# Splitting the 3x3 matmuls of convolutions 1 and 3 by row blocks, unshifted blocks first

## The chip, the cores and the metric

The kernel runs on one core of a Trainium2 chip. The metric is the time of one execution on the device, in microseconds, and the median of several runs is quoted. Besides the times there is one profiled execution, with a record of every instruction, DMA packet and semaphore update. All the readings below come from it.

A core has a matrix engine (TensorE, "PE" in the profile, with its weight loads under "PEld"), a vector engine (VectorE, "DVE"), an activation engine (ScalarE, "ACT"), a general engine (GpSimd, "POOL") and SyncE ("SP"), which here issues DMAs. Matmul results go to PSUM. Everything else lives in SBUF, which has 128 partitions.

## The reference

The input `x` has shape (8, 32, 128, 128). Two layers add to it. The first is a denoiser:

```
xb   = patch_match_stack(groupnorm(x))                   # 8 best shifted copies: 256 channels
dct  = conv(xb, dct_w, groups=32)
h    = relu(conv3x3_dw(conv1x1(xb, w1), w2))             # convolution 1
h    = relu(conv3x3_dw(conv1x1(h,  w3), w4))             # convolution 2
wien = sigmoid(conv3x3_dw(conv1x1(h, w5), w6))           # convolution 3
x    = x + conv1x1(conv(wien * dct, inv_dct_w, groups=32), agg_w)
```

`conv3x3_dw` is a 3x3 convolution that treats each of the 256 channels by itself, with a border of zeros. The second layer normalises again and adds a 5x5 convolution. The change concerns `conv3x3_dw` of convolutions 1 and 3.

## The kernel before, in words

**Tiles and steps.** An image is worked in 16 tiles of 8 rows (`R`), and a 17th short tile for the last rows, because each 3x3 convolution works one row behind its input. There are 8 x 17 = 136 steps (`steps`). In step `s` the kernel runs convolution 1 for tile `s`, convolution 2 for tile `s - 1`, convolution 3 for tile `s - 2` and the final stage for tile `s - 2`. Inside a step the loop goes `for i in (3, 2, 1, 0)`; 0 is the final stage. The same step also gathers pixels for later tiles and prepares the next image, whose VectorE tasks are dealt out by `tick`.

**Two halves of the channels.** Channels 128 to 255 take their 3x3 convolution on VectorE (`depthwise_v`, L695, nine taps). Channels 0 to 127 take it on TensorE (`depthwise_t`, L718), and that is the part that changes. Its 1x1 convolution (`pointwise_t`, L665) writes, through a ScalarE copy (L672), into the buffer `t`, one for each convolution, of 128 partitions x 4 channel groups x 4 slots x 128 columns. A partition stands for one of 4 rows and one of 32 channels. The ScalarE copy fills slots 2 and 3. A 3x3 convolution needs neighbouring rows on the partitions that one matmul contracts over, so slots 0 and 1 hold the same rows moved by half the partitions. DMAs on SyncE's queue fill them:

- L677, `t[64:P, :, 0:2] <- t[0:64, :, 2:4]`, of this tile;
- L679, `t[0:64, :, 1] <- t[64:P, :, 2]`, of this tile;
- L620 (`rows_before_t`), `t[0:64, :, 0] <- t[64:P, :, 3]`, issued after the convolution for the next tile.

**The matmuls.** `depthwise_t` reads `t` as two row blocks: block 0 is slots 0 and 1 (the shifted ones), block 1 is slots 2 and 3 (the unshifted ones). For each of two output offsets `u` (0 contracts over 96 partitions, 1 over 128), three column taps `dx` and four channel groups `j`, one matmul takes both blocks together, 2 x 2 x 128 = 512 columns (508 for the side taps). That makes 24 matmuls in the code; the trace shows each as two, 48 for one call. `pt[0]` and `pt[1]` are two PSUM buffers (`ps_dw`, one of each), read by two ScalarE activations (L731).

**Where a call stands.** `depthwise_t` is a generator. Its matmuls run at the first `next(dt)` of the iteration after its own, so that other work stands between the DMAs and their readers. On TensorE a full step goes: `pv3, p3, pg, | pv2, p2, pg, [3x3 of conv 3] | pv1, p1, pg, [3x3 of conv 2] | pc, pg, [3x3 of conv 1]`, where `pv` and `p` are the 1x1 convolutions (L641, L665), `pg` the gathered pixels (L603), `pc` the DCT (L777), and small pieces (`pd`, `pa`, `px`, `pt`) are put between. TensorE, VectorE and ScalarE run in exactly the order in which the code issues (`manual_schedule`). GpSimd's and SyncE's queues are ordered by the framework's scheduler.

Of the kernel before, what the change touches and what calls it, by code (L numbers as in the profile page):

```python
# [15 lines left out]
P = 128  # L16
C, K, H, W = 32, 8, 128, 128
# [3 lines left out]
NS = H // R  # L21
# [21 lines left out]
def bm3d_conv_preact(  # L43
# [16 lines left out]
    nc = tc.nc  # L60
# [49 lines left out]
    dwd = const.tile([P, 3, 2, 4, 3, C], F32, name="dwd")  # L110
# [36 lines left out]
    with tc.tile_pool(name="setup", bufs=1) as sp, tc.tile_pool(  # L147
# [23 lines left out]
        for name, w in (("w1", w1), ("w3", w3), ("w5", w5)):  # L171
            t = sp.tile([P, 2, CK], F32, name=f"nat_{name}", tag=f"nat_{name}")
            nc.sync.dma_start(t, w.rearrange("(m p) i a b -> p m (i a b)", p=P))
            if name == "w1":

                nat, t = t, sp.tile([P, 2, CK], F32, name="w1_kc")
# [439 lines left out]
    def rows_before_t(i, b, n):  # L616

        t = tb[i - 1]
        if n < NS:
            nc.sync.dma_start(t[0:64, :, 0], t[64:P, :, 3])  # L620
        else:
            nc.gpsimd.memset(t[0:64, :, 0], 0.0)
# [80 lines left out]
    def depthwise_t(i, b, n):  # L703
        t = tb[i - 1].rearrange("p q (h k) w -> p q h k w", k=2)
        nb = 2 if n < NS else 1

        pt = [
            ps_dw.tile([P, 2, 2, W], F32, name=f"pw{i}_{b}_{n}_{u}", tag=f"dw{u}")
            for u in range(2)
        ]  # L710

        nh = [2 if n < NS else (i + 1 - u) // 2 for u in range(2)]
        for u in range(2):
            hi = 96 if u == 0 else P
            for dx in (0, -1, 1):
                xa, xz = max(0, -dx), min(W, W - dx)
                for j in range(4 if nh[u] else 0):
                    nc.tensor.matmul(  # L718
                        pt[u][C * j : C * (j + 1), : nh[u], :nb, xa:xz],
                        dwd[0:hi, i - 1, u, j, dx + 1],  # L720
                        t[0:hi, j, : nh[u], :nb, xa + dx : xz + dx],
                        start=dx == 0,
                        stop=True,
                        skip_group_check=True,
                    )
        yield 1
        acc = accp.tile([P, R, W], F32, name=f"acc{i}_{b}_{n}_0", tag=f"acc{i}0")
        rows = acc.rearrange("p (k e) w -> p e k w", e=4)
        for u in range(2):
            if nh[u]:  # L730
                nc.scalar.activation(  # L731
                    rows[:, u : u + 2 * nh[u] - 1 : 2, :nb], pt[u][:, : nh[u], :nb], funcs[i - 1]
                )
        rows_before_t(i, b, n)
        accs[i, b, n][0] = acc
# [263 lines left out]
    with tc.manual_schedule(engines=ORDERED):  # L999
# [9 lines left out]
        u = 4  # L1009
# [5 lines left out]
        for s in range(len(steps) + 2):  # L1015
            if s < len(steps):
                b, n = steps[s]
# [8 lines left out]
            for i in (3, 2, 1, 0):  # L1026
# [6 lines left out]
                if live and i:  # L1033
                    src = source(i, bi, ni)
                    pointwise_v(i, bi, ni, lws[i - 1], src)
                    new_v, new_t = depthwise_v(i, bi, ni), depthwise_t(i, bi, ni)
                    accs[i, bi, ni] = [None, next(new_v)]
# [100 lines left out]
```

## Time and profile before

| | |
|---|---|
| median of 3 runs | 6862.14 us (6855.92 to 6876.67) |
| the profiled execution | 6856.73 us, of which the span from first to last instruction is 6855.0 us |
| PE busy | 6362.1 us, 93% of the span, 101,090 matmuls |
| DVE / ACT / POOL busy | 5857.0 us (85%) / 5067.7 us (74%) / 3250.0 us (47%) |
| granted TensorE clock, mean | 0.974 of full speed |
| 3x3 matmuls (L718) | 19,392, that is 408 calls of `depthwise_t` |
| DMA | 1019.84 MB, mean 149 GB/s |

"Busy" is the time in which an engine has an instruction running. A wait is put down to what came last. The chain of waits is followed back from the last instruction and shows what the end hung on. A line such as `L718` is a line of the kernel above. `pw<-t,dwd` says that the matmul writes `pw` and reads `t` and the weights `dwd`.

### The profile page before, as it was taken

Reading aid. Unit: us, or ns where it says so; the run is one execution under the profiler, and the core shown is the slowest. Engines: PE = TensorE matmul, PEld = TensorE weight load, DVE = VectorE, ACT = ScalarE, POOL = GpSimd, SP = SyncE. Lnnn points to the kernel's source line nnn. Section 1 sums busy time; section 2 is a strip of 40 time slices with the busy share of each in tenths; the row PEclk is TensorE's granted clock in tenths of the full one; section 3 lists DMA queues with packets and bytes.
Section 4 is the critical chain, followed back from the end, with each engine's and each line's share of the span. In section 5 each row is a group of like instructions: output and inputs, shape, how many; then the busy total and the mean of one; then the engine's idle time right before and its main releaser. Section 6 shows DMA issues by size and latency. Waiting matters only on the chain.

```text
span 6855.0 us, 232443 instructions
## 1 busy us (share of the span) xinstructions
PE 6362.1 (93%) x101090; PEld 2969.2 (43%) x101090; DVE 5857.0 (85%) x8822; ACT 5067.7 (74%) x6698; POOL 3250.0 (47%) x5351
## 2 busy tenths in 40 slices
PE   4698899999999999999999999999999999999997
PEld 1344444444444444444444444444444444444443
DVE  6799988989889898988989888898988889877776
ACT  4687768777687777877778777887768777786772
POOL 6345436544464444644446444464445544344334
PEclk9899999999999999999999999999999999999998
DMA  3566656666566675665656656566665666566553
GB/s 80 134 151 148 155 134 150 163 149 162 149 155 161 147 168 134 167 145 151 165 131 165 160 145 167 134 172 152 151 153 146 161 157 149 137 164 157 148 151 79
DMA packets 809531, 1019.84 MB, mean 149 GB/s; under 512 B 255456, under 2 KB 619936, under 8 KB 808512
## 3 DMA queue, kind: packets, MB, share of 16 engines
q0 software_dynamic: 422432, 745.61, 42.4%
q1 hardware_dynamic: 381056, 256.86, 16.9%
q8 instruction: 796, 13.04, 0.8%
q10 hardware_dynamic: 5024, 2.49, 0.2%
q14 instruction: 223, 1.83, 0.1%
HBM read 553.25 MB, written 217.01 MB: 112 GB/s over the span
## 4 chain that ended last, share of the span: by engine, by line
PE 53%; DVE 20%; DMA 9%; ACT 8%; issue 6%; POOL 3%; SPq 0%; ACTq 0%; POOLq 0%; DVEq 0%
PE pw L718 19%; PE pv L641 13%; DVE acc L695 13%; PE p L665 11%; DMA t<-t 4%; PE pg L603 3%; PE pc L777 2%; PE p L891 2%; DVE idx L506 2%; ACT ib L588 2%; DVE df L413 1%; PE pd L428 1%; ACT df L421 1%; PE pa L798 1%; DVE acc L785 1%
## 5 line engine op out<-in xcount | busy, mean ns | idle before, releaser
L695 DVE SCALAR_TENSOR_TENSOR acc<-tv,dwv,acc 128x1024 f32<-128x1024 f32 (+3 forms) x3264 | 4032.8, 1237 | 255.1 <-ACT acc L692 141.7
L718 PE MATMUL pw<-t,dwd 96*32 96x508 f32 (+6 forms) x19392 | 2161.7, 593 | 137.9 <-DMA t<-t 97.4
L574 POOL DMA_DIRECT2D ib<-idxd x1024 | 571.8, 559 | 1828.0 <-ACT sel L589 1677.2
L718 PEld LDWEIGHTS pw<-t,dwd 96*32 96x32 f32 (+1 forms) x19392 | 715.7, 112 | 1265.5 <-issue 1174.2
L588 ACT ACTIVATE ib<-ib,nplace 128x1024 bf16<-128x1024 bf16 x1024 | 1170.3, 1143 | 19.1 <-DMA ib<-idxd 19.1
L589 ACT ACTIVATE sel<-ib 128x1024 f32<-128x1024 bf16 x1024 | 1084.7, 1059 | 32.5
L665 PE MATMUL p<-acc,lw 128*32 128x256 f32 x16768 | 991.3, 381 | 20.0 <-ACT tv L649 19.5
L641 PE MATMUL pv<-acc,lw 128*128 128x512 f32 (+1 forms) x2112 | 972.0, 602 | 30.2 <-DVE acc L785 22.9
L758 POOL DMA_DIRECT2D xf<-xbd x1088 | 652.8, 634 | 305.3 <-PE pc L777 80.7
L665 PEld LDWEIGHTS p<-acc,lw 128*32 128x32 f32 x16768 | 556.6, 111 | 447.8 <-ACT tv L649 59.5
L649 ACT COPY tv<-pv 128x512 f32<-128x512 f32 (+2 forms) x784 | 439.2, 578 | 403.4 <-PE pv L641 380.6
L603 PEld LDWEIGHTS pg<-sel,xt 128*32 128x32 f32 x45056 | 575.3, 111 | 260.4 <-ACT sel L589 67.1
L421 ACT ACTIVATE df<-df 128x786 f32<-128x786 f32 (+2 forms) x576 | 468.5, 860 | 291.6 <-DVE df L413 288.5
L603 PE MATMUL pg<-sel,xt 128*32 128x48 f32 x45056 | 593.5, 207 | 89.2 <-ACT sel L589 47.6
L731 ACT ACTIVATE acc<-pw 128x512 f32<-128x512 f32 (+2 forms) x808 | 442.7, 573 | 295.7 <-PE pw L718 294.9
L641 PEld LDWEIGHTS pv<-acc,lw 128*128 128x128 f32 x2112 | 380.0, 191 | 524.3 <-issue 404.4
L413 DVE TENSOR_TENSOR df<-xn 128x786 f32<-128x786 f32 (+2 forms) x576 | 527.8, 968 | 82.8 <-PE pd L428 70.9
L699 ACT ACTIVATE acc<-acc 128x1024 f32<-128x1024 f32 (+3 forms) x408 | 416.9, 1022 | 235.4 <-DVE acc L695 235.1
L672 ACT COPY t<-p 128x512 f32<-128x512 f32 x800 | 424.7, 571 | 127.8 <-PE p L665 125.8
L692 ACT ACTIVATE acc<-tv,dwv 128x1024 f32<-128x1024 f32 (+3 forms) x408 | 454.6, 1114 | 57.9 <-PE pa L798 39.1
L641 PE MATMUL pv<-xb,lw 128*128 128x512 f32 x1024 | 474.5, 606 | 0.0
L665 PE MATMUL p<-xb,lw 128*32 128x256 f32 x8192 | 467.6, 380 | 0.0
(151 smaller groups left out, 5778.6 us busy)
## 6 DMA issues: line engine op xcount, KB each, us to landing
ib<-idxd POOLq DMA_DIRECT2D x1024, 256.0 KB, 4.5
xbd<-xb POOLq DMA_DIRECT2D x128, 1024.0 KB, 6.8
xf<-xbd POOLq DMA_DIRECT2D x960, 128.0 KB, 7.0
t<-t SPq DMA_DIRECT2D x792, 128.0 KB
t<-t SPq DMA_DIRECT2D x384, 256.0 KB
tv<-tv SPq DMA_DIRECT2D x384, 130.0 KB
xt<-xtd POOLq DMA_DIRECT2D x240, 176.0 KB, 4.4
xl<-xs POOLq DMA_DIRECT2D x256, 64.0 KB, 2.5
```

The source lines that it names most:

```text
L413: nc.vector.tensor_sub(df[:, :, ca:cz], xn[:, r0 : r0 + SR, ca:cz], xn[:, r0 + dy : r0 + dy + SR, ca + dx : cz + dx],)
L421: nc.scalar.activation(df[:, :, ca:cz], df[:, :, ca:cz], AF.Square)
L574: nc.gpsimd.dma_start(ib.rearrange("p k y x -> p (k y x)"), idxd[b][s4 // 8, s4 % 8, 4 * k0 : 4 * k0 + 8] .rearrange("k x -> (k x)") .part ...
L588: nc.scalar.activation(ib, ib, AF.Square, bias=nplace)
L589: nc.scalar.activation(sel, ib, AF.Relu, scale=-1.0, bias=1.0)
L603: nc.tensor.matmul(pg[C * j : C * (j + 1), :, xa:xz], xt[:, t], sels[j // 2][:, j % 2, :, xa:xz], start=True, stop=True,)
L641: nc.tensor.matmul(ps[:, :hr], lhsT[:, g, P:CK], src(g)[:, h : h + hr], start=g == 0, stop=g == 1,)
L665: nc.tensor.matmul(ps[C * r : C * (r + 1), e, :nb], lhsT[:, g, s], rows[:, r : r + 4 * nb - 3 : 4], start=g == 0, stop=g == 1,)
L692: nc.scalar.activation(acc, rows, AF.Copy, scale=tap)
L695: nc.vector.scalar_tensor_tensor(acc, rows, tap, acc, op0=ALU.mult, op1=ALU.add)
L718: nc.tensor.matmul(pt[u][C * j : C * (j + 1), : nh[u], :nb, xa:xz], dwd[0:hi, i - 1, u, j, dx + 1], t[0:hi, j, : nh[u], :nb, xa + dx : xz ...
L758: nc.gpsimd.dma_start(xf[p : p + C, m, j0:j1], src[g, m, (h + m + 1) % 2, :, :, ya:yz])
```

## The change

For convolutions 1 and 3 and full tiles (`n < NS`), the matmuls of a call are issued in two passes: first block 1 (slots 2 and 3) for both `u`, all `dx` and `j`; then block 0 (slots 0 and 1) in the same order. Each matmul has half the columns, 256 or 254, and each weight tile is loaded twice. Convolution 2 and the short last tiles stay in one pass.

```diff
         nh = [2 if n < NS else (i + 1 - u) // 2 for u in range(2)]
-        for u in range(2):
-            hi = 96 if u == 0 else P
-            for dx in (0, -1, 1):
-                xa, xz = max(0, -dx), min(W, W - dx)
-                for j in range(4 if nh[u] else 0):
-                    nc.tensor.matmul(
-                        pt[u][C * j : C * (j + 1), : nh[u], :nb, xa:xz],
-                        dwd[0:hi, i - 1, u, j, dx + 1],
-                        t[0:hi, j, : nh[u], :nb, xa + dx : xz + dx],
-                        start=dx == 0,
-                        stop=True,
-                        skip_group_check=True,
-                    )
+
+        parts = ((1, 2), (0, 1)) if i != 2 and n < NS else ((0, 2),)
+        for ka, kz in parts:
+            for u in range(2):
+                hi, kz = 96 if u == 0 else P, min(kz, nh[u])
+                for dx in (0, -1, 1):
+                    xa, xz = max(0, -dx), min(W, W - dx)
+                    for j in range(4 if kz > ka else 0):
+                        nc.tensor.matmul(
+                            pt[u][C * j : C * (j + 1), ka:kz, :nb, xa:xz],
+                            dwd[0:hi, i - 1, u, j, dx + 1],
+                            t[0:hi, j, ka:kz, :nb, xa + dx : xz + dx],
+                            start=dx == 0,
+                            stop=True,
+                            skip_group_check=True,
+                        )
         yield 1
```

## The prediction

> **What bounds the kernel now.** I read the page first: how full the engines are, and what the end hung on.
>
> ```profile
> span 6855.0 us, 232443 instructions
> PE 6362.1 (93%) x101090; PEld 2969.2 (43%) x101090; DVE 5857.0 (85%) x8822; ACT 5067.7 (74%) x6698; POOL 3250.0 (47%) x5351
> PE 53%; DVE 20%; DMA 9%; ACT 8%; issue 6%; POOL 3%; SPq 0%; ACTq 0%; POOLq 0%; DVEq 0%
> L718 PE MATMUL pw<-t,dwd 96*32 96x508 f32 (+6 forms) x19392 | 2161.7, 593 | 137.9 <-DMA t<-t 97.4
> ```
>
> TensorE is the bound: it is idle for 493 us, and 137.9 us of that lie before the 3x3 matmuls. The list of waits says for what, and what VectorE waits for meanwhile:
>
> ```profile
> DVE xr L806 <- PE pa L798: 311.8, 68, 15.7
> PE pw L718 <- DMA t<-t: 97.4, 39, 5.1
> ```
>
> Next the timeline, one row a call. First an undisturbed call, then a stalled one, then three short calls (last tiles of convolutions 1, 2 and 3):
>
> ```profile
> 2920.84 5.33 PE L718 MATMUL pw<-t,dwd 96*32 96x512 f32 x48
> 2934.24 8.32 PE L718 MATMUL pw<-t,dwd 96*32 96x512 f32 x48 [5.12 <-DMA t<-t]
> 3511.63 0.86 PE L718 MATMUL pw<-t,dwd 96*32 96x128 f32 x24
> 3545.05 1.51 PE L718 MATMUL pw<-t,dwd 96*32 96x128 f32 x48
> 3579.95 2.15 PE L718 MATMUL pw<-t,dwd 96*32 96x256 f32 x48
> ```
>
> The stalled call is idle for 5.12 us and then takes 8.32 us, not 5.33. The table by windows (busy time of PE, PEld, DVE, ACT, POOL, then granted clock, DMA share, GB/s) shows why, for this call, an undisturbed one, the step around it and the step after:
>
> ```profile
> 2934.24:2942.56 8.32, 8.32 (x49) 2.23 (x49) 6.56 (x21) 5.24 (x6) 6.60 (x11) 0.63 0.77 224
> 2920.84:2926.17 5.33, 5.33 (x60) 1.78 (x55) 5.19 (x6) 4.48 (x6) 2.43 (x2) 1.00 0.47 78
> 2896.00:2960.00 64.00, 55.83 (x849) 25.35 (x851) 55.64 (x89) 45.41 (x58) 28.60 (x47) 0.95 0.59 145
> 2960.00:3010.00 50.00, 49.99 (x796) 22.80 (x792) 44.71 (x74) 37.82 (x50) 25.86 (x38) 1.00 0.60 131
> ```
>
> After the wait the clock is 0.63, not 1.00. Without a stall (last row) TensorE has no gap at all. The chain of waits, around another stall of convolution 3, shows what is late:
>
> ```profile
> 3002.86 10.75 DMA t<-t
> 3013.61 1.15 issue
> 3014.76 7.03 PE pw L718 x48
> ```
>
> The DMA that fills slots 0 and 1 took 10.75 us, more than the work put between it and its reader.
>
> [...]
>
> **The change, part by part.**
>
> *Split matmuls.* 256 calls (2 convolutions x 8 images x 16 tiles) get 48 more matmuls in the trace each, 12,288, and as many weight loads. The short calls price them. 24 matmuls of 128/127 columns take 0.86 us, 48 take 1.51: 27 ns each and 0.21 us of tail. In the 2.15 us call, 24 have 254/256 columns: (2.15 - 0.21 - 24 x 0.027) / 24 = 53.8 ns. A full one costs (5.33 - 0.21) / 48 = 106.7 ns. So a split call takes 96 x 53.8 + 210 = 5.37 us instead of 5.33, and 256 calls cost **+9 us**. The weight loads are in these durations. At four times the rate, `pg` does 88 matmuls with their loads in 1.09 us, so the issue rate does not bind.
>
> *Wait moved.* In the compiled order the first 48 matmuls of a call lose the wait on SyncE's DMAs, and matmul 49 has it. What remains at the front is the ScalarE copy into slots 2 and 3, which precedes the DMA, and the release of PSUM by the previous call's L731. In the timeline that release ends 0.8 to 20 us before TensorE runs dry at these stalls. So a stall of g shrinks to max(0, g - 2.67), half of 5.33 being worked first. I added up the timeline rows of full tiles with over 0.15 us idle. Convolution 1: 19 stalls, 53.9 us, ten over 2.67 with 15.7 us beyond. Convolution 3: 29 stalls, 60.3 us, nine over, 4.6 us beyond. Removed: 38.2 + 55.7 = **-94 us**. (The rest of 137.9 is convolution 2's 17 us, 5 us in the last tiles, and gaps inside calls.)
>
> *Clock.* The same 48 calls take 64 us more than 48 x 5.33. Of the remaining gaps six are over 1.5 us; those before of 1.5 us and less mostly left a call at 5.33. I let 14 us stay: **-50 us**. Bounds: 0[...] and -64.
>
> *ScalarE.* L731 of `u = 0` can start after 72 of 96 matmuls, about 4.0 us into the call instead of 2.7; the next in its queue is L731 of `u = 1`, which waits for the end (the trace shows ScalarE idle there for 1.97 us). Nothing: cover 1.3 us after a copy of 0.6. If it went, 0.6 us a call.
>
> *Queues.* VectorE's and ScalarE's order is unchanged, SyncE's has one swap in the first tiles. L620 still waits for the call's end, behind it on SyncE is L627, as before. GpSimd's order moves: some 420 of 5356 instructions, nearly all by one to three places (92 `ib` loads, 63 `xr` loads, five image loads 14 places earlier, one 13 later). `ib` feeds ScalarE's `sel`, and that `pg`. TensorE now waits for `sel` for 67 + 48 us (loads and matmuls, overlapping); I bound the shift by a quarter of 67, ±15 us, and take 0.
>
> *Where the stall goes.* Gross: -94 - 50 + 9 = -135 us. Next late is VectorE: in the 64 us step it is busy 55.64, and the gain there is 2.67 (a 3.05 us stall of convolution 3) + 2.67 + 2.99 (the call above) = 8.3, so it would be full. Such steps (tile 4) come in six images; if VectorE cannot fall behind into the easier next step (44.71 of 50), some 4 us each are lost, about 20 with partial cover elsewhere. In the same steps the second stall's DMA shares engines with loads that TensorE does not pace; its landing may stay put, and the first stall's gain returns as a longer second wait: 4 pairs x 2.5 = 10 us. A further 5 us for new waits. Net: -135 + 35 = **-100 us**. Against the profiled execution's 6856.7 (span 6855.0 and 1.7 around it) that is 6757; it lies 5 us under the median, so I forecast **6762 us**.
>
> **Rivals.**
>
> *A. As above*, 6725 to 6800: chance 0.66.
>
> *B. The stall moves.* Landing times are set by the DMA backlog and VectorE fills, so that the gaps are half saved (-47), the clock stays low (0), the split costs +9: 6824; with half the clock too, 6799. For it: DMA share 0.77 to 0.79 at stalls. Against it: VectorE waits 311.8 us for `pa` alone, so it has room. Chance 0.22, 6800 to 6841.
>
> *C. No difference:* GpSimd's new order costs 15 us on top of B: 6839, or the DMAs run later by what was won. The change does do what it says, the compiled order shows it. Chance 0.06.
>
> *D. Slower: the price of a matmul.* [...] It decides from 144 / 12,288 = 11.7 ns each. Against it: the short calls give 9 us / 12,288 = 0.7 ns. They have the same columns and strides as the split ones, though on 96 partitions only for the 254-wide; the 128-partition half-width shape is not in the trace. Chance 0.06.
>
> **Numbers.** Range 6715 to 6830: the low end is the whole of both gains, -94 - 64 + 9 = -149; the high end is B's 6824 with a little of the queue's bound. About 0.1 lies on each side. A measurement can tell about 0.3%, 21 us: faster means under 6841 (A and B, 0.88), same 0.06, slower 0.06.
>
> **What would show it.** L718's rows: 31,680 matmuls, idle before them from 137.9 to about 45 us, of which convolution 2's 17 stay; stalls inside the call, before the block-0 matmuls, 15 to 25 in number, none over about 3 us. Undisturbed split calls: 5.37 us in the timeline. Mean granted clock 0.974 to about 0.98. TensorE busy 6362 - 50 + 9, about 6320. New waits, if any, should name VectorE or `sel`. I am wrong if split calls take over 5.9 us (D), if the inner stalls sum to more than 60 us (B), or if idle before `pg` grows by as much as L718's falls.

## The result and the profile after

| | before | after |
|---|---|---|
| median of 8 runs each | 6873.4 us (6855.9 to 6884.7) | 6837.0 us (6821.8 to 6846.2) |
| ratio | | 0.995, 95% interval 0.9935 to 0.9965 |
| span of the profiled execution | 6855.0 us | 6842.1 us |

The change saves 36 us of the 100 us forecast. 6837 lies outside the range of 6715 to 6830, where rival B had put its time. The profiled execution of before lies at the low end of its runs and that of after at the high end, so the two traces differ by only 13 us. Sums over the traces below are held against 13 us, comparisons of kernels against ratios of runs. Lines of the kernel move by 3: L718 is now L721, L777 is L780, L785 is L788, L798 is L801, L806 is L809.

The page of after: the lines that answer to those shown of before, and the queue that carries instructions (packets, MB, share). The last row has busy time, mean ns of one matmul, then idle time before them and what ended most of it.

```profile
span 6842.1 us, 257025 instructions
PE 6347.0 (93%) x113378; PEld 3356.7 (49%) x113378; DVE 5856.0 (86%) x8822; ACT 5064.5 (74%) x6698; POOL 3241.3 (47%) x5351
q8 instruction: 892, 14.61, 0.9%
PE 17%; DVE 3%; DMA 1%; ACT 1%; issue 1%; POOL 0%; SPq 0%; POOLq 0%; DVEq 0%; ACTq 0%
L721 PE MATMUL pw<-t,dwd 96*32 96x254 f32 (+7 forms) x31680 | 2143.5, 421 | 89.7 <-issue 41.9
```

TensorE does 12,288 matmuls more and is yet busy 15 us less. Idle before the 3x3 matmuls falls from 137.9 to 89.7 us, where about 45 were forecast, and what ends most of it is no longer a DMA but "issue", that is, no wait that the profile shows. (The chain covers only 23% of the span here and is of no use.) The waits of after (us in total, times, the longest), then two of before:

```profile
PE pw L721 <- issue: 41.9, 30, 4.7
PE pc L780 <- DVE acc L788: 38.5, 8, 6.3
PE pv L641 <- DVE acc L788: 31.2, 19, 2.2
PE pw L721 <- DMA t<-t: 27.2, 18, 4.2
...
DVE xr L809 <- PE pa L801: 288.0, 65, 14.1
```

```profile
PE pw L718 <- issue: 20.5, 12, 4.0
...
PE pv L641 <- DVE acc L785: 22.9, 15, 2.2
```

The wait for `t` falls from 97.4 to 27.2 us as meant. In its place "issue" doubles, and a wait of 38.5 us before the DCT's matmuls is there that before does not have. VectorE still waits 288.0 us for `pa`: it has not filled up. The timeline of after shows what this means for single calls (start, duration, tiles, count, and in brackets the idle time before and what ended it). Its first two rows are the two halves of the call that was idle for 5.12 us and took 8.32; then a call of convolution 3 that stops; then an undisturbed call.

```profile
2926.64 2.77 PE L721 MATMUL pw<-t,dwd 96*32 96x256 f32 x48
2929.94 2.79 PE L721 MATMUL pw<-t,dwd 96*32 96x256 f32 x48 [0.53 <-DMA t<-t]
...
3003.14 0.61 PE L721 MATMUL pw<-t,dwd 96*32 96x256 f32 x7
3008.47 7.28 PE L721 MATMUL pw<-t,dwd 96*32 96x256 f32 x89 [4.72 <-issue]
...
3060.05 5.35 PE L721 MATMUL pw<-t,dwd 96*32 96x256 f32 x96
```

The first call works as planned: half of it covers the DMA, and 0.53 us are left. The second has nothing to wait for after 7 matmuls (`t` is awaited at the 49th), and stops for 4.72 us all the same. The windows of after (columns as in the prediction: TensorE first, near the end the granted clock, the DMA share and GB/s) give the first call, the stop of the second, and the two parts of what follows it:

```profile
2926.64:2932.73 6.09, 5.56 (x117) 3.26 (x105) 6.02 (x7) 0.63 (x2) 1.61 (x3) 1.00 0.53 122
3003.75:3008.47 4.72, 0.00 (x1) 0.00 (x1) 4.62 (x5) 3.84 (x5) 2.65 (x5) 0.75 1.04 202
3008.47:3012.90 4.43, 4.43 (x44) 2.60 (x47) 4.29 (x5) 0.00 (x0) 1.45 (x4) 0.50 0.72 169
3012.90:3015.75 2.85, 2.85 (x53) 1.60 (x43) 2.78 (x3) 0.60 (x1) 2.85 (x6) 1.00 0.62 194
```

During the stop the profile has its 16 DMA engines busy throughout (the share is 1.04; it counts whole packets that start in the stretch, so it can pass 1), and the clock then stays at 0.50 for 4.43 us. The first call, idle for 0.53 us inside, keeps a clock of 1.00.

What is late? The queue "instruction" on the page moved 892 packets of 16,384 bytes, 796 before. The 24,576 instructions that the split adds (12,288 matmuls, 12,288 weight loads) are 96 times 256, which is just the difference. The totals agree: the trace of before has 203,815 instructions on TensorE (its loads and semaphore instructions with them), 796.2 times 256, that of after 228,382, 892.1 times. So TensorE's instructions arrive by DMA in blocks of 256. I counted TensorE's instructions in the trace from its start and looked where in a block of 256 its idle time of over 0.15 us without a shown wait ends (start and end of the kernel left out):

```
                 all such idle time    at counts 193 and 194 of 256
before           44.0 us,  35 stalls   23.3 us,  23 stalls
after            70.4 us,  56 stalls   62.1 us,  49 stalls
```

The increase stands at one place of the block. In after, all 49 stalls at this place end within 2.2 us of the landing of a packet of that queue, with a median of 1.40 us, and each time it is the very packet whose turn it is: with the queue's packets numbered from 1, its number is the number of whole 256s counted, in all 49, and in the 23 of before. (The count begins with the trace, so where in it a block has its edge is not shown.)

Two more readings of the same traces bear on why a block comes late. In the 3 us before these 49 landings the DMA engines are 0.87 busy on average, before the landings of all packets of the queue 0.59. And no packet of after, beyond the start, begins more than 301 of TensorE's instructions before the count at which its own block is due, so a block is on its way hardly more than one block ahead.

The other new wait, in VectorE's and TensorE's timeline of after, and TensorE's of before at the same work:

```profile
2811.09 9.21 DVE L695 SCALAR_TENSOR_TENSOR acc<-tv,dwv,acc 128x1024 f32<-128x1024 f32 x7
2813.07 1.29 PE L780 MATMUL pc<-xf,ldct 64*64 64x128 f32 x10
2820.22 0.48 DVE L788 TENSOR_TENSOR acc<-acc,pc 128x128 f32<-128x128 f32 x2
2820.56 1.98 PE L780 MATMUL pc<-xf,ldct 64*64 64x512 f32 x6 [6.20 <-DVE acc L788]
```

```profile
2821.38 1.29 PE L777 MATMUL pc<-xf,ldct 64*64 64x128 f32 x10
2823.70 1.08 PE L777 MATMUL pc<-xf,ldct 64*64 64x512 f32 x6 [1.03 <-ACT tmp_b L270]
```

In the first tile of an image the DCT works two row groups, one of a single row (64x128) and one of four rows (64x512), with two PSUM tiles `pc` each. The last of these four tiles, called the second DCT tile below, used to wait 1.03 us for ScalarE. Now it waits 6.20 us for VectorE's product (L788) with the first row group, which stands behind 9.21 us of taps (L695). This comes in six images, 6.20 to 6.35 us each. The compiled order has the same: in before the second tile waits for ScalarE, in after for VectorE in just these six places, though the diff does not touch this code. The tiles share five PSUM buffers (`ps_x`), so the framework seems to have given this one another of the five than before; that is inferred from the waits, and why it did so, nothing here shows.

### The profile page after: what moved, and what is told of

Same layout as the page of the kernel before. It is cut to its first block, busy times and chain, and to the rows that moved or that the text cites. A ratio compares the mean times of both kernels' runs of the same rounds, so it can differ in the third digit from the quotient of the medians.

```text
span 6842.1 us, 257025 instructions
## 1 busy us (share of the span) xinstructions
PE 6347.0 (93%) x113378; PEld 3356.7 (49%) x113378; DVE 5856.0 (86%) x8822; ACT 5064.5 (74%) x6698; POOL 3241.3 (47%) x5351
## 5 line engine op out<-in xcount | busy, mean ns | idle before, releaser
L695 DVE SCALAR_TENSOR_TENSOR acc<-tv,dwv,acc 128x1024 f32<-128x1024 f32 (+3 forms) x3264 | 4032.3, 1237 | 250.1 <-ACT acc L692 139.0
L721 PE MATMUL pw<-t,dwd 96*32 96x254 f32 (+7 forms) x31680 | 2143.5, 421 | 89.7 <-issue 41.9
L721 PEld LDWEIGHTS pw<-t,dwd 96*32 96x32 f32 (+1 forms) x31680 | 1107.0, 111 | 908.4 <-issue 437.1
L641 PE MATMUL pv<-acc,lw 128*128 128x512 f32 (+1 forms) x2112 | 973.5, 603 | 35.8 <-DVE acc L788 31.2
L603 PEld LDWEIGHTS pg<-sel,xt 128*32 128x32 f32 x45056 | 576.2, 111 | 262.4 <-ACT sel L589 67.1
L734 ACT ACTIVATE acc<-pw 128x512 f32<-128x512 f32 (+2 forms) x808 | 440.6, 573 | 256.4 <-PE pw L721 255.5
```

The costliest lines, as they stand in the source:

```text
L603: nc.tensor.matmul(pg[C * j : C * (j + 1), :, xa:xz], xt[:, t], sels[j // 2][:, j % 2, :, xa:xz], start=True, stop=True,)
L641: nc.tensor.matmul(ps[:, :hr], lhsT[:, g, P:CK], src(g)[:, h : h + hr], start=g == 0, stop=g == 1,)
L695: nc.vector.scalar_tensor_tensor(acc, rows, tap, acc, op0=ALU.mult, op1=ALU.add)
L721: nc.tensor.matmul(pt[u][C * j : C * (j + 1), ka:kz, :nb, xa:xz], dwd[0:hi, i - 1, u, j, dx + 1], t[0:hi, j, ka:kz, :nb, xa + dx : xz + dx ...
```

## The experiments

The expectations use these names. B: the new wait of `pc`, put down to its buffer, costs what the trace shows. I: instructions that arrive late cost the rest. P, or the price, or the sum: only the split matmuls' own duration counts. "Exchange" is the edit of the first experiment.

**1. The buffer.** The products of the first DCT tile are issued after those of the second, so that the second cannot be made to wait for the first. The work is the same; the compiled order then waits for ScalarE again, as before does.

```diff
+        late = []
...
-            for m in range(2):
-                nc.vector.tensor_mul(acc[m][:, a:z], acc[m][:, a:z], pc[m][:, : z - a])
+            def products(a=a, z=z, pc=pc):
+                for m in range(2):
+                    nc.vector.tensor_mul(acc[m][:, a:z], acc[m][:, a:z], pc[m][:, : z - a])
+
+            late.append(products)
+            if n or r0:
+                while late:
+                    late.pop()()
```

With the split:

> The changed kernel, but in the first tile of an image the two products of the DCT's second row group are issued on VectorE before those of the first; the same work, and the compiled order then has the second DCT tile wait for ScalarE again, as in the kernel before, and not for VectorE. Theory B (buffer): the wait of about 6.3 us before L780 in six images is 38 us of lost gain: it is gone and the time falls by 25 to 40 us against the changed kernel, to a ratio of 0.989 to 0.992 against before. Rival (absorbed): VectorE is what is late there, the wait reappears before another TensorE line in the same step, and the ratio stays at 0.995.

Without it, the exchange alone, on the kernel before:

> The kernel before with the same exchange of products in the first tile and nothing else, a control for it. Both theories: no difference, ratio 1.000 within 0.002; no wait of TensorE for VectorE's product before L777's second row group.

Measured: with the split **0.9885** (0.9867 to 0.9903), 6792.5 us; alone 1.0001 (0.9988 to 1.0013). The timeline of the split with the exchange, at the same place:

```profile
2802.68 1.29 PE L781 MATMUL pc<-xf,ldct 64*64 64x128 f32 x10
2804.93 1.08 PE L781 MATMUL pc<-xf,ldct 64*64 64x512 f32 x6 [0.96 <-ACT tmp_b L270]
```

The wait is gone, and the ratio falls from 0.995 to 0.9885: 0.0065 of 6863 us, 45 us. Since the exchange gives nothing by itself, those 45 us are what the changed wait costs the split kernel. 38.5 - 6.6 = 32 us of them are the wait itself (6.6 us is the old wait, six times); the remainder of 13 us is within the noise of the two ratios, some 16 us.

**2. The instructions alone.** With the exchange, but the shifted block first. Each call has the same 96 matmuls and waits for `t` at the first, as before.

```diff
-        parts = ((1, 2), (0, 1)) if i != 2 and n < NS else ((0, 2),)
+        parts = ((0, 1), (1, 2)) if i != 2 and n < NS else ((0, 2),)
```

> The matmuls split as in the changed kernel, but the shifted row block first, so that the early start is undone and the price of the split alone remains; with the exchange of products, so that the DCT's wait is out of it. Prediction's step (9 us for the split): ratio 1.001. Theory I (instruction supply: 24,576 more TensorE instructions, which have to be fetched by DMA and run dry when the DMA engines are full): 1.005 to 1.010, with idle time inside the 3x3 calls that the profile puts down to issue of 50 us or more, against 20.5 before, and waits on DMA t<-t as before, 90 us or more.

Measured: **1.0023** (1.0014 to 1.0033), some 16 us. Both forecasts missed; it lies between. Its waits:

```profile
PE pw L721 <- DMA t<-t: 117.8, 50, 5.0
...
PE pw L721 <- issue: 31.3, 21, 4.0
```

The waits for the DMA are back, and idle time without a wait inside the calls of convolutions 1 and 3 is 24.4 us (1.6 in before), less than after's 40.7 in the same calls. So part of the late instructions comes with their number, and more of it shows once TensorE no longer waits for `t`. A reading that fits is that the waiting gave the block time to arrive; no run tests this apart. The order of the two passes is worth 1.0023 - 0.9885 = 0.0138, 95 us.

**3. Which calls.** Only 56 of the 256 calls are split, those of the tiles that stalled most. Their compiled order keeps ScalarE's wait, so no exchange is needed.

```diff
+SPLIT = {(1, 4), (1, 7), (3, 2), (3, 4), (3, 7), (3, 8), (3, 15)}
...
-        parts = ((1, 2), (0, 1)) if i != 2 and n < NS else ((0, 2),)
+        parts = ((1, 2), (0, 1)) if (i, n) in SPLIT else ((0, 2),)
```

> Split, unshifted first, only for the tiles at which the kernel before stalled in most images: convolution 1 tiles 4 and 7, convolution 3 tiles 2, 4, 7, 8 and 15, that is 56 calls of 256. The compiled order has no wait for VectorE before the DCT's second row group. Theory I: the runs-dry stalls fall back to about the level of before (20 to 30 us before the 3x3 matmuls), most of the DMA waits are still covered, ratio 0.985 to 0.989, faster than the exchange of products alone by 15 us or more. Rival (the split costs next to nothing, so only covered stalls count): the ratio is no better than that of the full split with the exchange of products, 0.990 or more.

Measured: **0.9888** (0.9871 to 0.9905). The waits before its 3x3 matmuls:

```profile
PE pw L722 <- DMA t<-t: 37.6, 22, 5.0
...
PE pw L722 <- issue: 25.9, 16, 4.3
```

The ratio is in the range of theory I, but not 15 us below the full split with the exchange: with 22% of the added instructions the gain is the same. Idle time without a wait in the calls is 18.0 us, against 44.9 with all 256; the waits that the unsplit calls keep (26 us at the front) use up that difference.

**4. Each convolution alone**, with the exchange: `i == 3` and `i == 1` in the place of `i != 2`.

> Only convolution 3 split, unshifted first, with the exchange of products (no wait of TensorE for VectorE in the DCT's second row group). The full split with the exchange gave 0.9885. Theory of the sum as predicted (gaps of 55.7 us and half of the clock's 31 us): ratio 0.988 to 0.990. Theory I (late instruction blocks take the place of the waits that are removed, above all in convolution 3, whose inner gaps outside the wait were 29 us in the changed kernel): 0.993 to 0.996.

> Only convolution 1 split, unshifted first, with the exchange of products. Theory of the sum as predicted (gaps of 38.2 us and clock of up to 33 us): 0.991 to 0.993. Theory I, by which convolution 1 loses little to late instruction blocks (10 us inside its calls in the changed kernel): the same, 0.991 to 0.994; so convolution 1 alone gains as much as convolution 3 or more, where the prediction had it gain less.

Measured: convolution 3 alone **0.9951** (0.9939 to 0.9964), convolution 1 alone **0.9931** (0.9904 to 0.9957). The product is 0.9882; both together had 0.9885, so the gains just add. The prediction gave convolution 3 the larger share of the waits (55.7 of 94 us), yet it gains no more; which of the two gains more, the overlapping intervals leave open. The traces show what works against convolution 3. With it alone, its front waits go from 60.3 to 0.6 us, but 29.9 us of idle time without a wait arise inside its calls (before: 1.6). With convolution 1 alone that is 4.4 us inside the split calls.

**5. Four times the instructions.** With the exchange; each call in four passes, a quarter of the columns each, the shifted block first, so that 36,864 matmuls are added in the place of 12,288.

```diff
-        parts = ((1, 2), (0, 1)) if i != 2 and n < NS else ((0, 2),)
-        for ka, kz in parts:
+        parts = ((0, 1, 0, 1), (0, 1, 1, 2), (1, 2, 0, 1), (1, 2, 1, 2))
+        parts = parts if i != 2 and n < NS else ((0, 2, 0, nb),)
+        for ka, kz, ra, rz in parts:
...
-                            pt[u][C * j : C * (j + 1), ka:kz, :nb, xa:xz],
+                            pt[u][C * j : C * (j + 1), ka:kz, ra:rz, xa:xz],
...
-                            t[0:hi, j, ka:kz, :nb, xa + dx : xz + dx],
+                            t[0:hi, j, ka:kz, ra:rz, xa + dx : xz + dx],
```

> Convolutions 1 and 3 split in four parts of a quarter each (128 or 127 columns), shifted blocks first, with the exchange of products: the same columns and no earlier start, but three times the added instructions of the half split, whose price was a ratio of 1.0023. By the price of a matmul of this width in the profile before (27.25 ns): 192 x 27.25 + 210 = 5.44 us a call, 28 us in all, ratio 1.004. Theory I: each 256 instructions are one 16 KB block, 1084 in place of 796, and the idle time that the profile puts down to issue grows with them, to 90 us or more; ratio 1.010 to 1.020.

Measured: **1.0355** (1.0325 to 1.0385), 236 us more, above every forecast. The page, and the timeline of one undisturbed call and of one that stops:

```profile
q8 instruction: 1083, 17.74, 1.1%
...
L722 PE MATMUL pw<-t,dwd 96*32 96x127 f32 (+3 forms) x56256 | 2250.8, 314 | 323.7 <-issue 259.4
```

```profile
2718.39 5.43 PE L722 MATMUL pw<-t,dwd 96*32 96x128 f32 x192
...
2935.73 0.38 PE L722 MATMUL pw<-t,dwd 96*32 96x128 f32 x2
2939.50 3.69 PE L722 MATMUL pw<-t,dwd 96*32 96x128 f32 x128 [3.39 <-issue]
2943.52 1.94 PE L722 MATMUL pw<-t,dwd 128*32 128x127 f32 x62 [0.33 <-issue]
```

Undisturbed, 192 matmuls of a quarter's columns take 5.43 us, just 0.1 us more than 48 whole ones: 0.7 ns for each added matmul. So the 11.7 ns for each that rival D needs are not paid here, with the four channel groups in turn, even at 127 columns. Most of the loss is idle time: 259.4 us without a wait before these matmuls, 20.5 in before. Of all 303 us of such stalls, 295 stand at counts 193 and 194 of 256, 230 stalls out of 237. Three times the added instructions cost far more than three times as much. A reason that fits is the time left for a block to arrive: TensorE works through 384 instructions in 5.43 us, a block of 256 in 3.6 us, where in halves it takes 7.1.

**6. Shifted blocks.** The split with the exchange, and one extra pass in the very first call, so that all later instructions move by 96 places in their blocks.

```diff
         parts = ((1, 2), (0, 1)) if i != 2 and n < NS else ((0, 2),)
+        parts = parts[:1] + parts if (i, b, n) == (1, 0, 0) else parts
```

> The split with the exchange of the products, and the unshifted pass of the very first call of convolution 1 issued twice (48 more matmuls and 48 more weight loads, once, with the same result), so that all later TensorE instructions stand 96 places further in their blocks of 256. Theory I (TensorE stops because its next block of instructions has not been fetched): over 80% of the idle time that no wait explains stays at the counts 193 and 194 within a block, and so falls on other matmuls than without the shift; under a third of the stalls recur at the same matmul. Rival (a wait of that place in the work which the profile doesn't show): the stalls stay at the same matmuls, and their counts move by 96, to 33 and 34. Time in both: as without the shift, within 25 us.

Measured, one run: 6792.9 us. Stalls of over 0.4 us without a wait, found again at the same matmul (two more or fewer allowed) of the split with the exchange:

```
                              at counts 193, 194    of these at the same matmul
after (no shift)              43                    29
shifted by 96                 36                     0
```

Of all stalls over 0.15 us, 60.5 of 67.1 us stay at counts 193 and 194; nothing turns up at 33 and 34. This rules out an unseen wait of a certain matmul: the stalls follow the blocks and leave the work. Together with the packets that land shortly before each ends, each the one whose turn it is, theory I is shown for these stalls.

**7. A better choice of calls.** Two kernels on one chip: the 56 calls of the third experiment again, and 96, with those tiles added that still waited there, convolution 2's tile 15 among them.

```diff
+SPLIT = {(1, 0), (1, 4), (1, 6), (1, 7), (1, 12), (2, 15)} | {(3, n) for n in (2, 4, 6, 7, 8, 15)}
```

> Only the 56 calls that stalled most are split, once more, as the measure for the kernel with 96 such calls on the same chip: 0.987 to 0.991 of the time before in both theories.

> 96 calls are split: the 56 and, of those that still wait, convolution 1 in tiles 0, 6 and 12, convolution 2 in tile 15 and convolution 3 in tile 6 (some 32 us of waits, of which the split can hide up to 2.67 us each, about 28). Theory I (a split pays where the call waits, and costs instructions alone where it doesn't): 15 to 30 us less than with 56 calls, a ratio to before of 0.984 to 0.987. Rival (what is taken away comes back as the next late transfer or block of instructions): within 8 us of the 56 calls, 0.988 to 0.991.

Measured: 56 calls **0.989** (0.9863 to 0.9916), 6792.2 us (6790.0 to 6797.5); 96 calls **0.9843** (0.9805 to 0.9882), 6765.2 us (6738.4 to 6781.4). The difference is 27 us, within theory I's 15 to 30; the intervals of the ratios touch, but no run of the one kernel reaches those of the other. The page of the kernel with 96 calls:

```profile
q8 instruction: 832, 13.63, 0.9%
...
L722 PE MATMUL pw<-t,dwd 128*32 128x508 f32 (+7 forms) x24000 | 2126.9, 502 | 60.4 <-issue 28.2
```

Idle time before these matmuls is 60.4 us, less than half of before's 137.9 and less than the 74.7 with 56 calls, with 37.5% of the change's added instructions. This is the fastest kernel of the study, some 100 us under before and 70 under the change as made.

## Why the prediction was wrong

**Split matmuls: the price right, the sentence on issue wrong.** Undisturbed calls take 5.35 us (5.37 forecast; the terms as printed add up to 5,375 ns and so to 11 us, not 9), and quarters confirm 0.7 ns a matmul. The step that failed is its last sentence: "the issue rate does not bind". It was argued from `pg`, 88 matmuls with their loads in 1.09 us. Such a burst is 176 instructions, shorter than one block of 256, and says nothing of how the next block comes. In after, idle time without a wait inside the calls of convolutions 1 and 3 is 40.7 us; 1.9 us of it stand at a 49th matmul and are counted with the waits for the DMA below, which leaves 37 more than before. Some 20 of these calls are also, at full clock, 0.50 to 0.66 us longer than their idle time explains; all told, 21 us more than before is neither idle nor slow clock. I put this down to late instructions too, since the calls that do not cross counts 193 and 194 have only 1.3 us of the excess; up to 3 us of it lie in calls that stop for the DMA alone. Late instructions thus cost 55 to 58 us, where the sum has nothing.

**Wait moved: right.** Front waits of full tiles went from 114.3 to 0.2 us. Inner waits for the DMA are 11.7 us (convolution 1) and 12.9 us (convolution 3), 24.6 against 20.3 forecast, 17 in number against 15 to 25. Saved: 90 us, forecast 94. So the DMAs did not land later by what was won, as rivals B and C had it.

**Clock: right for these calls.** Half clock cost the calls of convolutions 1 and 3 67 us in before and 23 in after (time in the calls at half speed, without the idle time, halved): 44 saved, 50 forecast. One stop for instructions can bring it back: after the 4.72 us above the clock was 0.50 for 4.43 us.

**ScalarE: nothing seen against it.** Its idle time before these activations (L731, now L734) fell from 294.9 to 255.5 us.

**Queues: this step failed.** "VectorE's and ScalarE's order is unchanged" is true and was not enough. The step compared the order of instructions; it did not compare what each instruction waits for. TensorE's wait before the second DCT tile changed from ScalarE to VectorE. Measured: 32 us in the trace, 45 us between kernels, where the step allowed ±15 us, and those for GpSimd's order alone. It was to be seen in the compiled order before any run.

**Where the stall goes: mis-sized.** It allowed 35 us for VectorE, coupled stalls and new waits. VectorE gave 8 us more in the waits of `pv` (22.9 to 31.2 us); it did not fill up.

The sum, in the traces: -90 (waits) - 44 (clock) + 4 (split) = -130 us, forecast -135. Against it stand +37 and +21 (instructions), +32 (`pc`), +8 (`pv`) and some +8 of small waits for ScalarE and without cause before `pd`, `p` and `pg`: +106 where the forecast has +35. That leaves -24; the spans differ by 13, and the last 11 us lie in other lines and are not taken apart.

Rival B's time came true by another mechanism: its gaps were not half saved but nearly wholly, and its inner stalls of over 60 us did not come. Rival C's queue was POOL's; the harm came on TensorE's own waits. Rival D needed 11.7 ns a matmul where 0.7 were measured in undisturbed calls, but its direction, that the number of instructions costs time, is what the quarters show.

## What to carry to other kernels

Count the instructions that a change adds as transfers too: in this kernel each 256 of TensorE's came by DMA, as a packet of 16,384 bytes, and the late ones came where the DMA engines were 0.87 busy. So split only the calls that wait, as far as this kernel goes: 96 calls gave 1.6%, all 256 gave 0.5%, and 1.15% with the buffer put right. Before a run, compare the waits in the compiled order as well as the order, also at instructions that the diff does not touch: a changed wait far from the edit took away more than half of the gain (45 of 79 us).

## What the runs showed of the hardware that I had not expected

- TensorE stood still for up to 4.72 us (6.75 us in the split with the exchange) with nothing to wait for but its own instructions, although the packets of these take 0.9% of the DMA engines' time. In the kernel before 23 us went this way already. In after, past the start, a block's packet starts at most 301 instructions before that block is due.
- The cost of added instructions is far from linear: 12,288 matmuls with their loads cost 16 us (1.3 ns each, waits kept), 36,864 cost 236 us (6.4 ns each).
- These matmuls get cheaper nearly in proportion to their columns down to 127: with four channel groups in turn, an undisturbed call takes 5.33, 5.35 and 5.43 us in 48, 96 and 192 of them.
